# Reordering both ends of a two-layer attention kernel: query and key blocks in turns, timetables of their own for three sequences, and a last tree in two halves

## The chip, the core and the metric

The kernel runs on one core of a Trainium2 chip. The metric is the device time of one execution in microseconds (us). Five engines work side by side, each through its own queue in program order: PE (TensorE, matmuls; PEld in the profile is its weight load), DVE (VectorE), ACT (ScalarE), POOL (GpSimd) and SP (SyncE, which here issues all DMA transfers).

## What is computed

The input is x, 8 sequences of 512 tokens with 256 features, all float32. Two layers follow each other, each an attention and a soft decision tree, both with a residual:

```python
x = x + attn_a(layernorm(x))   # 16 heads of 16, with biases, no mask
x = x + ffn(layernorm(x))
x = x + attn_b(layernorm(x))   # 16 heads of 16, rotary positions, causal
x = x + ffn(layernorm(x))

def ffn(x):                    # a tree of depth 8: 255 inner nodes, 256 leaves
    q = einsum('btd,ed->bte', x, Wq)
    gate = sigmoid(q @ routers.T)
    leaf_prob = product of the gates, or of one minus them, along each path
    return einsum('btd,ed->bte', leaf_prob @ leaf_values, Wout_w) + Wout_b
```

## The kernel before

**Sequences and steps.** The kernel counts sixteen sequences: 0 to 7 are the batch in the first layer, 8 to 15 the same batch in the second (causal) layer. A sequence has 32 ticks (`STEPS`): four groups of four heads, four steps in each group, two ticks per step. In one step (the loop at L655) the program writes, in this order, the transposed scores of one block of 128 keys and their exponentials (`scores`, tiles `st` and `pt`), and the row maxima of one block of 128 queries that are needed seven steps later (`maxima`, tiles `mx` and `most`; `LEAD` is 14 ticks). After the fourth step of a group, `weigh` multiplies the exponentials by the values (`av`). The maxima of four steps are negated and transposed (`less`, `lessT`), and moved to the tile `m`, from which a third matmul adds them to the scores.

**Banks.** All matmul results go to eight PSUM banks that are handed out in turn. A step takes four for `st` and four for `mx`, so the next scores need banks that the exponentials on ACT, and the reductions on DVE, have let go.

**Fillers.** Everything else is put between these steps by a small planner (`Units`). A generator yields the kind of its next piece and the tick from which it is due: "big" and "small" are PE pieces (pulled once per step, after `weigh`), "v" is DVE, "g" POOL (both pulled twice), "d" a DMA, "row" the transposed maxima. A piece that is due is written at the next pull of its kind, the oldest due time first. The engines' queues then hold exactly the order of the program (`in_program_order`). The due times come from two tables: `BEFORE` (what a sequence needs before its steps, relative to its own start) and `BEHIND` (what follows its attention, relative to the next sequence's start), each with one entry for the first layer and one for the causal layer.

**Before its steps** (`pre`, L355), a sequence loads x (`x`), takes the statistics (`stats`, DVE), normalizes (`norm`, POOL: L284 to L292, tile `xn`), transposes (`xt`), and makes queries and keys in two blocks of 128 features each (`q`, `k`, L403). In the first layer ACT writes each block twice, as float32 (`r`) and rounded (`hl`, first half), and `halves` (L329) subtracts them for the second half of `hl` (`q_halves`, `k_halves`). `move` then issues four DMAs for a query block and two for a key block, of 256 KB each, which bring the features of a head together in the tiles `q` and `k`. `hl` has two buffers. The values (`v`) and the residual's bias (`bias`, POOL) follow.

**Behind its steps**, `spread` moves the outputs and the softmax sums, `divide` (L542) makes the reciprocals, sends them through DRAM and back (`apart`, `den`), and multiplies (L555). `post` makes the output projection (`y`), which is added to x (L562), and `tree` (L578) the rest: statistics, norm (`xnt`), transposes (`txt`), gates (`z`, `th`), the products down the tree (`levels`, tile `lp`, two DVE instructions for each of eight levels), transposes (`lt`), the leaf product (`ty`) and the store. A tree takes up to two sequences' time, so those of two sequences are in flight together.

**At the start**, sequence 0 runs through `pre` alone, then its values, then its moves; the four products of the tree's constant weights (`chains`, tiles `wg` and `wl`) begin at tick 2, and the value bias is folded into the output bias (`fold_bias`) at the end of `pre`. **At the end**, the planner is drained one tick at a time (L680).

Of the kernel before, what the change touches and what calls it, by code (L numbers as in the profile page):

```python
# [41 lines left out]
F32 = mybir.dt.float32  # L42
# [6 lines left out]
P = 128  # L49
B, S, D = 8, 512, 256  # L50
H, HD = 16, 16
# [17 lines left out]

BEFORE = (  # L70
    dict(x=-41, stats=(-39, -39), norm=(-34, -34, -34), xt=(-33, -29), q=(-29, -27), k=(-27, -27),
         q_halves=(-27, -27), k_halves=(-23, -23), v=(-13, -13, -11, -11), bias=(-12, -6)),
    dict(x=-43, stats=(-42, -39), norm=(-37, -37, -37), xt=(-33, -33), q=(-29, -27), k=(-19, -19),
         q_turn=(-25, -22), q_round=-20, q_halves=(-20, -20), k_turn=(-18, -17), k_round=-17,
         k_halves=(-17, -17), v=(-13, -13, -9, -9)),
)
BEHIND = (
    dict(y=(11, 11, 15, 15), stats=(15, 18), norm=(18, 18, 18), xt=(23, 23), z=(27, 29, 29, 29),
         bias=(30, 30), levels=(31, 32, 39, 39, 39, 41), lt=(43, 53), ty=(63, 63, 67, 67)),
    dict(y=(13, 13, 15, 15), stats=(18, 19), norm=(19, 19, 20), xt=(25, 27), z=(29, 29, 29, 29),  # L80
         bias=(20, 25), levels=(30, 30, 31, 34, 40, 40), lt=(47, 51), ty=(53, 53, 63, 69)),
# [3 lines left out]
OUTPUT = (3, 1, 2, 1, 3)  # L85

# [47 lines left out]
def hybrid_kernel(ctx, tc, x, a_qk, a_v, a_o, a_qk_b, a_v_b, a_o_b, b_q, b_k, b_v, b_o,  # L134
# [33 lines left out]
    def store_x(n):  # L168
        dst = between[n] if n < B else out[n - B]
        nc.sync.dma_start(dst.rearrange("(t p) d -> p t d", p=P), xs.pop(n))  # L170
# [8 lines left out]
    for m in ms:  # L179
# [23 lines left out]
        for w, n, tag in ((f_q, "f_q", "lpT"), (f_routers, "f_routers", "th"),  # L203
                          (f_values, "f_values", "lp"), (f_out, "f_out", "den"))
# [22 lines left out]
    units = Units()  # L227
    wg = const.tile([P, NC, NODES], F32, tag="wg", name="wg")
    wl = const.tile([P, NC, D], F32, tag="wl", name="wl")

    def chains():


        for to, left, right in ((wg, raws[0], raws[1]), (wl, raws[2], raws[3])):
            n = to.shape[2]
            for m in range(NC):
                ps = bank([P, D], f"w{n}_{m}")
                for k in range(NC):
                    nc.tensor.matmul(
                        ps[:, :n], lhsT=left[:, k, m * P : (m + 1) * P], rhs=right[:, k, :],  # L240
                        start=k == 0, stop=k == NC - 1,
                    )
                if to is wl:
                    nc.vector.tensor_scalar(to[:, m, :], ps[:, :n], leaf_scale[:, m : m + 1], None, ALU.mult)
                else:
                    nc.scalar.copy(to[:, m, :], ps[:, :n])
                yield "big", units.now + 2

    def fold_bias():

        vb = pool1.tile([P, NC, P], F32, tag="lp1", name="vb")
        for c in range(NC):
            nc.vector.tensor_copy(vb[:, c, :], v_b[:, c : c + 1].to_broadcast([P, P]))
        ps = bank([P, D], "vbo")
        for c in range(NC):
            nc.tensor.matmul(ps, lhsT=vb[:, c, :], rhs=wa.o[:, c, :], start=c == 0, stop=c == NC - 1)
        nc.vector.tensor_tensor(out_b, ps, out_b, ALU.add)

    def before(n, name):

        return shifted(BEFORE[n >= B][name], n)

    def behind(n, name):

        return shifted(BEHIND[n >= B][name], n + 1)
# [5 lines left out]
    def layer_norm(n, name, when, got):  # L271

        x = xs[n]
        stats = pool2.tile([P, NT, 6], F32, tag="ln_stats", name=f"ln_stats{name}")
        mv = pool2.tile([P, NT, 2], F32, tag="ln_mv", name=f"ln_mv{name}")
        for t in range(NT):
            if t == 2:
                yield "v", when(n, "stats")[1]
            nc.vector.bn_stats(stats[:, t, :], x[:, t, :])
            nc.vector.bn_aggr(mv[:, t, :], stats[:, t, :])  # L280
        times = when(n, "norm")
        yield "g", times[0]
        less_mean = pool2.tile([P, NT], F32, tag="ln_less", name=f"ln_less{name}")
        nc.gpsimd.tensor_scalar(less_mean, mv[:, :, 0], -1.0, None, ALU.mult)  # L284
        rstd = pool2.tile([P, NT], F32, tag="ln_rstd", name=f"ln_rstd{name}")
        nc.gpsimd.tensor_scalar(rstd, mv[:, :, 1], EPS, None, ALU.add)
        nc.gpsimd.tensor_tensor(rstd, rstd, neg_half, ALU.pow)
        xn = pool2.tile([P, NT, D], F32, tag="xn", name=f"xn{name}")
        for t in range(NT):
            if t % 2 == 0:  # L290
                yield "g", times[1 + t // 2]
            nc.gpsimd.tensor_scalar(  # L292
                xn[:, t, :], x[:, t, :], less_mean[:, t : t + 1], rstd[:, t : t + 1], ALU.add, ALU.mult
            )
        got.append(xn)

    def add_bias(n, bias, times):
        for t in range(0, NT, 2):
            part = xs[n][:, t : t + 2, :]
            nc.gpsimd.tensor_tensor(part, part, bias.unsqueeze(1).to_broadcast([P, 2, D]), ALU.add)  # L300
            if t == 0:
                yield "g", times[1]
# [8 lines left out]
    def by_tokens(srcT, w, n, name, evict, times):  # L311


        t = 0
        while t < NT:
            if t:
                yield "big", times[t]
            count = 2 if t < NT - 1 and times[t] == times[t + 1] else 1
# [8 lines left out]
            t += count  # L327

    def halves(raw, hl, which, n, c):  # L329


        on = nc.vector if n >= B else nc.gpsimd
# [20 lines left out]
        moves.setdefault(n, []).append(units.add(move(), "d", units.now + 1))  # L353

    def pre(n):  # L355
# [33 lines left out]
        vals[n] = units.add(by_tokens(xnT, w.v, D, f"v{n}", values, times), "big", times[0])  # L389
        for which, name in enumerate("qk"):  # L390
# [3 lines left out]
            for c in range(NC):  # L394
                yield "big", before(n, name)[c]
                if not which and not c:

                    assert before(n, name)[0] > (n - 1) * STEPS + LEAD
                    qs[n] = [pool2.tile([P, NG, S], F32R, tag=f"q{i}", name=f"q{i}_{n}") for i in range(2)]
                    ks[n] = pool2.tile([P, NG, S], F32R, tag="k", name=f"k{n}")  # L400
# [7 lines left out]
                if causal:  # L408

                    for i, table in enumerate((cos, sin) if c == 0 else (sin, cos)):  # L410
                        raws.append(pool1.tile([P, S], F32, tag=f"r{c}{i}", name=f"r{n}{which}{c}{i}"))
                        nc.vector.tensor_tensor(raws[-1], ps, table, ALU.mult)
                else:
                    raws.append(pool1.tile([P, S], F32, tag=f"r{which}{c}", name=f"r{n}{which}{c}"))
                    at = 2 * which + c
                    for to in (raws[c], hls[c][:, 0, :]):
                        nc.scalar.activation(to, ps, AF.Identity, bias=w.qk_b[:, at : at + 1])  # L417
# [10 lines left out]
        if n == 0:  # L428
            fold_bias()

# [111 lines left out]
    def divide(n, c):  # L542
# [11 lines left out]
        yield "g", units.now + OUTPUT[4]  # L554
        nc.gpsimd.tensor_tensor(outT[:, c, :], outT[:, c, :], den, ALU.mult)  # L555
# [10 lines left out]
    def post(n):  # L566
# [9 lines left out]
        yield from tree(n)  # L576

    def tree(n):  # L578

        got = []
        yield from layer_norm(n, f"t{n}", behind, got)
        xn = got[0]
        for c in range(NC):
            yield "small", behind(n, "xt")[c]
            if c == 0:
                xnT = pool2.tile([P, NC, S], F32, tag="xnT", name=f"txnT{n}")
            transposed(xnT, xn, c, f"txt{n}_{c}")
        times = behind(n, "bias")  # L590
        biases[n] = units.add(add_bias(n, f_bias, times), "g", times[0])
        yield "big", behind(n, "z")[0]
        if n:
            units.finish(trees[n - 1], lambda: paths[0] == n - 1)
        th = pool1.tile([P, NT, LEAVES], F32, tag="th", name=f"th{n}")
# [6 lines left out]
        yield from by_tokens(xnT, wg, NODES, f"z{n}", gates, behind(n, "z"))  # L602

        lp = None
        times = deque(behind(n, "levels"))
        for level in range(DEPTH):
            m = 1 << level
            for side, one in enumerate((-1.0, 1.0)):
                if level == DEPTH - 1 or (side == 0 and level in (0, 3, 5, 6)):
                    yield "v", times.popleft()  # L610
                if side == 0:
                    if level == DEPTH - 1 and n:
                        units.finish(trees[n - 1], lambda: paths[1] == n - 1)
                    new = pool1.tile([P, NT, 2 * m], F32, tag=f"lp{level % 2}" if level < DEPTH - 1 else "lp",
                                     name=f"lp{n}_{level}")
                    pairs = new.rearrange("p t (n s) -> p t n s", s=2)
                    of_level = th[:, :, m - 1 : 2 * m - 1]
                if lp is None:
                    nc.vector.tensor_scalar(pairs[:, :, :, side], of_level, one, None, ALU.add)
                else:  # L620
                    nc.vector.scalar_tensor_tensor(  # L621
                        pairs[:, :, :, side], of_level, one, lp, ALU.add, ALU.mult
# [3 lines left out]
        for c in range(NC):  # L626
            yield "small", behind(n, "lt")[c]
            if c == 0:
                if n:
                    units.finish(trees[n - 1])  # L630
                lpT = pool1.tile([P, NC, S], F32, tag="lpT", name=f"lpT{n}")
            transposed(lpT, lp, c, f"lt{n}_{c}")
        paths[1] = n
        yield "big", behind(n, "ty")[0]
        yield from by_tokens(lpT, wl, D, f"ty{n}", to_x(n), behind(n, "ty"))
        yield "d", units.now + 2
        units.finish(biases.pop(n))
        store_x(n)
# [11 lines left out]
    units.finish(vals.pop(0))  # L650
    for move in moves.pop(0):
        units.finish(move)
    units.add(chains(), "big", 2)
# [99 lines left out]
```

## Time and profile before

| What | us |
|---|---|
| median of three runs | 1194.44 |
| lowest and highest | 1192.46, 1198.91 |
| profiled execution, its own time | 1199.47 |
| its span, from the first to the last instruction | 1197.8 |
| PE busy in the span | 1089.3 (91%) |
| DVE busy | 842.1 (70%) |
| ACT busy | 639.8 (53%) |
| POOL busy | 405.9 (34%) |
| first matmul of the maxima | 28.30 |
| first matmul of the scores | 47.01 |
| last copy of an attention output (`o`) begins | 1152.77 |
| last addition to x begins | 1193.47 |

All times of the trace are counted from the start of the span. A busy engine is one that has an instruction under way; a matmul's end is modelled, so a busy PE isn't PE at its peak. The granted clock is the share of PE's full clock in a stretch: it is a mean of pieces at 1.0 and at 0.5. Where a line of the timeline or of the chain of waits has a bracket, it is the idle time of the engine before that instruction, and what ended it.

The distance from one sequence's first exponential to the next one's is some 70 to 74 us in the first layer and 66 to 72 in the causal layer; from the first one of sequence 15 to the end of its last it is 51.7 us.

### The profile page before, as it was taken

Reading aid. Unit: us, or ns where it says so; the run is one execution under the profiler, and the core shown is the slowest. Engines: PE = TensorE matmul, PEld = TensorE weight load, DVE = VectorE, ACT = ScalarE, POOL = GpSimd, SP = SyncE. Lnnn points to the kernel's source line nnn. Section 1 sums busy time; section 2 is a strip of 40 time slices with the busy share of each in tenths; the row PEclk is TensorE's granted clock in tenths of the full one; section 3 lists DMA queues with packets and bytes.
Section 4 is the critical chain, followed back from the end, with each engine's and each line's share of the span. In section 5 each row is a group of like instructions: output and inputs, shape, how many; then the busy total and the mean of one; then the engine's idle time right before and its main releaser. Section 6 shows DMA issues by size and latency. Waiting matters only on the chain. (4 is left out here: it accounts for less than half of the span.)

```text
span 1197.8 us, 24647 instructions
## 1 busy us (share of the span) xinstructions
PE 1089.3 (91%) x8916; PEld 619.1 (52%) x8916; DVE 842.1 (70%) x2384; ACT 639.8 (53%) x1451; POOL 405.9 (34%) x636
## 2 busy tenths in 40 slices
PE   5999999999999999999998999999989988899966
PEld 3434354555535545454554555555564645555544
DVE  2866487777767777777767787777878777776723
ACT  2266667666657566665663544545453544544431
POOL 4121223232422214232233443435453543434332
PEclk9689999999999999999998999989999999989988
DMA  8020302104141131411302214031312313030110
GB/s 285 6 112 21 120 21 82 56 16 143 38 138 39 35 116 39 143 60 38 133 18 108 74 38 148 32 124 33 134 49 80 103 34 143 30 126 16 41 50 35
DMA packets 69658, 91.52 MB, mean 76 GB/s; under 512 B 15008, under 2 KB 36256, under 8 KB 69536
## 3 DMA queue, kind: packets, MB, share of 16 engines
q1 hardware_dynamic: 69536, 89.94, 21.7%
q8 instruction: 70, 1.15, 0.4%
q14 instruction: 52, 0.43, 0.1%
HBM read 20.71 MB, written 8.91 MB: 25 GB/s over the span
## 5 line engine op out<-in xcount | busy, mean ns | idle before, releaser
L499 ACT ACTIVATE pt<-st 128x512 f32<-128x512 f32 (+3 forms) x1024 | 446.8, 523 | 198.5 <-PE st L436 195.1
L463 DVE TENSOR_REDUCE most<-mx 128x1 f32<-128x512 f32 x512 | 317.3, 683 | 134.8 <-PE mx L436 134.6
L458 DVE CUSTOM_DVE_ANT_0 seen<-mx,mask 128x384 f32<-128x384 f32 (+3 forms) x512 | 251.0, 490 | 123.4 <-PE mx L436 66.9
L436 PE MATMUL mx<-k,q 32*128 32x512 f32 (+3 forms) x2048 | 241.1, 400 | 42.1 <-DMA k<-hl 9.0
L515 PE MATMUL av<-pt,v 128*32 128x512 f32 (+3 forms) x2048 | 213.6, 561 | 5.7 <-ACT pt L499 3.8
L436 PE MATMUL st<-q,k 32*128 32x512 f32 (+3 forms) x2048 | 198.5, 410 | 1.6 <-ACT pt L499 0.8
L502 POOL TENSOR_SCALAR_AFFINE_SELECT pt<-pt 128x256 f32<-128x256 f32 x256 | 105.4, 424 | 278.4 <-ACT pt L499 274.4
L436 PEld LDWEIGHTS mx<-k,q 32*128 32x128 f32 x2048 | 136.3, 187 | 107.5 <-DVE x L562 22.6
L436 PEld LDWEIGHTS st<-q,k 32*128 32x128 f32 x2048 | 94.3, 186 | 114.6 <-issue 73.4
L515 PEld LDWEIGHTS av<-pt,v 128*32 128x32 f32 x2048 | 65.6, 117 | 141.9 <-issue 109.4
L520 ACT COPY o<-av 128x512 f32<-128x512 f32 x64 | 37.6, 587 | 161.4 <-issue 124.3
L436 PE MATMUL st<-m,ones 32*128 32x512 f32 (+3 forms) x1024 | 104.1, 358 | 0.0
L333 POOL TENSOR_TENSOR hl<-r,hl 128x512 fp32r<-128x512 f32 x32 | 41.5, 1297 | 166.1 <-ACT hl L417 166.1
L621 DVE SCALAR_TENSOR_TENSOR lp<-th,lp 128x8 f32<-128x8 f32 (+6 forms) x224 | 66.8, 336 | 2.6
L555 POOL TENSOR_TENSOR out<-out,den 128x512 f32<-128x512 f32 x32 | 41.6, 1299 | 76.0 <-DMA den<-apart 73.9
L322 PE MATMUL z<-wg,txnT 128*128 128x255 f32 x256 | 63.6, 396 | 3.0 <-ACT pt L499 2.6
L403 PE MATMUL qk<-xnT,b_qk 128*128 128x512 f32 x128 | 64.4, 638 | 1.5 <-ACT pt L499 0.8
L403 PE MATMUL qk<-xnT,a_qk 128*128 128x512 f32 x128 | 64.6, 636 | 0.2
L322 PE MATMUL ty<-wl,lpT 128*128 128x256 f32 x256 | 63.8, 388 | 0.5 <-ACT lpT L309 0.2
L436 PEld LDWEIGHTS st<-m,ones 32*128 32x128 f32 x1024 | 59.4, 187 | 5.7
L284 POOL TENSOR_SCALAR ln_lesst<-ln_mvt 128x4 f32<-128x4 f32 x16 | 3.8, 239 | 162.6 <-DVE ln_mvt L280 162.6
L322 PEld LDWEIGHTS z<-wg,txnT 128*128 128x128 f32 x256 | 47.5, 194 | 15.1 <-ACT pt L499 7.1
(76 smaller groups left out, 1136.5 us busy)
## 6 DMA issues: line engine op xcount, KB each, us to landing
q<-hl SPq DMA_DIRECT2D x128, 256.0 KB
k<-hl SPq DMA_DIRECT2D x64, 256.0 KB
out<-o SPq DMA_DIRECT2D x64, 128.0 KB
den<-apart SPq DMA_DIRECT2D x32, 256.0 KB
x<-x SPq DMA_DIRECT2D x8, 512.0 KB
between<-x SPq DMA_DIRECT2D x8, 512.0 KB
x<-between SPq DMA_DIRECT2D x8, 512.0 KB
out<-x SPq DMA_DIRECT2D x8, 512.0 KB
```

The source lines that it names most:

```text
L322: nc.tensor.matmul(ps[:, i, :n], lhsT=srcT[:, c, (t + i) * P : (t + i + 1) * P], rhs=w[:, c, :], start=c == 0, stop=c == NC - 1,)
L333: on.tensor_tensor(hl[:, 1, :], raw, hl[:, 0, :].bitcast(F32), ALU.subtract)
L403: nc.tensor.matmul(ps, lhsT=wt[:, k, c * P : (c + 1) * P], rhs=xnT[:, k, :], start=k == 0, stop=k == NC - 1,)
L436: nc.tensor.matmul(ps, lhsT=lhsT, rhs=rhs, start=i == 0, stop=i == len(operands) - 1)
L458: nc.vector.tensor_tensor_reduce(out=seen[:, :width], in0=ps[:, :width], in1=mask[:, S - width :], scale=1.0, scalar=LOWEST, op0=ALU.add, ...
L463: nc.vector.tensor_reduce(at, ps, AX.X, ALU.max)
L499: nc.scalar.activation(pt[:, i, : S - first], ps[:, : S - first], AF.Exp, scale=SCALE)
L502: nc.gpsimd.affine_select(out=pt[:, :, :P], in_=pt[:, :, :P], pattern=[[0, 2], [1, P]], compare_op=ALU.is_ge, fill=0.0, base=0, channel_mu ...
L515: nc.tensor.matmul(av[32 * j : 32 * j + 32, first:], lhsT=vs[n % 2][:, kt, g * NJ + j, :, :].rearrange("p d s -> p (d s)"), rhs=pts[j // 2 ...
L520: nc.scalar.copy(o4, av)
L555: nc.gpsimd.tensor_tensor(outT[:, c, :], outT[:, c, :], den, ALU.mult)
L621: nc.vector.scalar_tensor_tensor(pairs[:, :, :, side], of_level, one, lp, ALU.add, ALU.mult)
```

## The change

**Start.** `pre(0)` makes the blocks in the order q0, k0, q1, k1, and each is moved as soon as it is made. The second blocks' `hl` lie in the two buffers of `out`, so four buffers serve. The key blocks' subtraction goes to DVE. The norm of sequence 0 is on DVE, but for the power (still POOL). The values of sequence 0 are no longer finished ahead of the loop; they have ticks 7, 7, 11 and 11. `fold_bias` (its copies now on POOL) and the four weight products move from the start to the ticks 25, 27, 29, 43 and 49.

**Timetables.** Sequences 0 and 1 get entries of their own in `BEFORE`; several due times of the two common entries change. Sequence 14 gets its own entry in `BEHIND`, and the halves of sequence 15 one each.

**End.** For sequence 15 the division is done by DVE in two halves of 256 tokens. Each half starts its own `last`: projection, statistics, norm, one bank of transposes for its two tiles, gates, levels, leaf product and store. The second half has tiles of its own, in buffers of `hl`, `r` and `out`.

```diff
+LAST = 2 * B - 1
 BEFORE = (
-    dict(x=-41, stats=(-39, -39), norm=(-34, -34, -34), xt=(-33, -29), q=(-29, -27), k=(-27, -27),
-         q_halves=(-27, -27), k_halves=(-23, -23), v=(-13, -13, -11, -11), bias=(-12, -6)),
-    dict(x=-43, stats=(-42, -39), norm=(-37, -37, -37), xt=(-33, -33), q=(-29, -27), k=(-19, -19),
-         q_turn=(-25, -22), q_round=-20, q_halves=(-20, -20), k_turn=(-18, -17), k_round=-17,
-         k_halves=(-17, -17), v=(-13, -13, -9, -9)),
+    dict(x=-47, stats=(-39, -39), norm=(-34, -34, -34), xt=(-33, -29), q=(-29, -27), k=(-27, -27),
+         q_halves=(-27, -27), k_halves=(-27, -27), v=(-13, -13, -11, -11), bias=(-16, -10)),
+    dict(x=-43, stats=(-42, -42), norm=(-39, -37, -37), xt=(-33, -33), q=(-29, -27), k=(-19, -19),
+         q_turn=(-26, -24), q_round=-20, q_halves=(-20, -20), k_turn=(-18, -17), k_round=-17,
+         k_halves=(-17, -17), v=(-11, -11, -9, -9)),
+    dict(x=-41, stats=(-41, -39), norm=(-37, -32, -32), xt=(-31, -31), q=(-29, -27), k=(-23, -19),
+         q_halves=(-23, -23), k_halves=(-19, -19), v=(-13, -11, -5, -3), bias=(-8, 6)),
+    dict(v=(-7, -7, -3, -3), bias=(13, 18)),
 )
 BEHIND = (
-    dict(y=(11, 11, 15, 15), stats=(15, 18), norm=(18, 18, 18), xt=(23, 23), z=(27, 29, 29, 29),
-         bias=(30, 30), levels=(31, 32, 39, 39, 39, 41), lt=(43, 53), ty=(63, 63, 67, 67)),
-    dict(y=(13, 13, 15, 15), stats=(18, 19), norm=(19, 19, 20), xt=(25, 27), z=(29, 29, 29, 29),
-         bias=(20, 25), levels=(30, 30, 31, 34, 40, 40), lt=(47, 51), ty=(53, 53, 63, 69)),
+    dict(y=(11, 11, 15, 15), stats=(15, 18), norm=(18, 18, 19), xt=(23, 23), z=(27, 29, 29, 29),
+         bias=(30, 34), levels=(31, 32, 36, 39, 39, 41), lt=(43, 53), ty=(63, 63, 67, 67)),
+    dict(y=(13, 13, 15, 15), stats=(18, 19), norm=(23, 23, 23), xt=(25, 27), z=(29, 29, 29, 29),
+         bias=(18, 30), levels=(30, 30, 31, 34, 39, 41), lt=(47, 51), ty=(53, 53, 63, 69)),
+    dict(y=(5, 5, 15, 15), stats=(15, 15), norm=(15, 15, 16), xt=(19, 23), z=(27, 27, 31, 31),
+         bias=(20, 25), levels=(31, 31, 32, 34, 40, 40), lt=(47, 47), ty=(53, 53, 63, 63)),
+    dict(y=(15, 15), stats=18, norm=(18, 21), xt=21, z=(29, 29), bias=28,
+         levels=(29, 29, 35, 38, 38, 38), lt=43, ty=(49, 49)),
+    dict(y=(19, 19), stats=20, norm=(21, 28), xt=29, z=(39, 39), bias=39,
+         levels=(46, 46, 47, 47, 48, 48), lt=51, ty=(53, 53)),
 )
+CHAINS = (25, 27, 29, 43, 49, 49)
...
     def before(n, name):
-        return shifted(BEFORE[n >= B][name], n)
+        table = BEFORE[(3, 2)[n] if n < 2 else n >= B]
+        return shifted(table[name] if name in table else BEFORE[0][name], n)
     def behind(n, name):
-        return shifted(BEHIND[n >= B][name], n + 1)
+        return shifted(BEHIND[2 if n == LAST - 1 else n >= B][name], n + 1)
...
+        on = nc.vector if name == "n0" else nc.gpsimd
...
     def halves(raw, hl, which, n, c):
-        on = nc.vector if n >= B else nc.gpsimd
+        on = nc.vector if n >= B or (n == 0 and which) else nc.gpsimd
...
+        if n == 0:
+            queries_and_keys(n)
+            for c in range(NC):
+                for which in range(2):
+                    raw, hl = block(w, xnT, which, c, "out" if c else "hl")
+                    halves(raw, hl, which, n, c)
+                    units.finish(moves[n][-1])
+            return
...
-        if n == 0:
-            fold_bias()
...
+        if n == LAST and c == NC - 1:
+            for half in range(2):
+                part = slice(half * S // 2, (half + 1) * S // 2)
+                nc.vector.tensor_tensor(outT[:, c, part], outT[:, c, part], den[:, part], ALU.mult)
+                units.add(last(half), "big", shifted(BEHIND[3 + half]["y"], n + 1)[0])
+            return
...
+    def transposed_half(dst, src, ts, name):
+        ps = bank([P, NC, 2, P], name)
+        for c in range(NC):
+            for i, t in enumerate(ts):
+                nc.tensor.transpose(ps[:, c, i, :], src[:, t, c * P : (c + 1) * P], ident)
+        nc.scalar.copy(dst[:, :, ts[0] * P : ts[0] * P + 2 * P], ps.rearrange("p c t q -> p c (t q)"))
...
+    def last(half):
+        ts = range(2 * half, 2 * half + 2)
+        def when(n, name):
+            return shifted(BEHIND[3 + half][name], n + 1)
+        yield from by_tokens(outs[LAST][0], wb.o, D, f"y{LAST}", to_x(LAST), when(LAST, "y"), ts)
+        yield "v", when(LAST, "stats")
+        yield from tree(LAST, when, ts)
...
     units.finish(pres.pop(0))
-    units.finish(vals.pop(0))
-    for move in moves.pop(0):
-        units.finish(move)
-    units.add(chains(), "big", 2)
+    moves.pop(0)
+    units.add(chains(), "big", CHAINS[0])
```

## The prediction

> **What bounds the kernel now.** I read the page's 40 slices first, then the busy time by stretches, then the timeline of the first 50 us, one step of the first sequence, and the chain of waits from the last softmax to the end. In the slices the matmul engine is at nine tenths or more except at both ends.
>
> ```profile
> PE   5999999999999999999998999999989988899966
> PEclk9689999999999999999998999989999999989988
> ```
>
> The second row is the granted clock in tenths. The middle is PE-bound at nearly full clock; idle time that a new order can fill lies at the two ends. The start, in the timeline (start, length, engine, line, work, and in brackets the idle time before it and what ended it):
>
> ```profile
> 23.64 0.69 ACT L417 ACTIVATE hl<-qk,a_qk_b 128x512 fp32r<-128x512 f32 x1 [3.14 <-DMA q<-hl]
> 24.35 4.58 SPq L346 DMA_DIRECT2D k<-hl  x4
> 28.30 1.21 PE L436 MATMUL mx<-k,q 32*128 32x512 f32 x16 [2.50 <-DMA k<-hl]
> ```
>
> The first key block is written at 23.64 because `hl` has two buffers and both hold queries that are still being moved; its moves leave from 24.35, and the first maxima start at 28.30, when they land. Then the lead, and the cold steps after it:
>
> ```profile
> 28.30:47.00 18.70, 15.70 (x77) 8.56 (x77) 17.49 (x36) 1.00 (x3) 6.22 (x10) 0.72 0.08 29
> 47.00:57.00 10.00, 10.00 (x49) 5.85 (x49) 7.86 (x15) 5.56 (x11) 0.00 (x0) 0.50 0.01 2
> ```
>
> Columns: stretch, its length, busy us of PE, weight loads, DVE, ACT, POOL, granted clock, DMA share, GB/s. In the lead DVE is busy 17.49 of 18.70 us: it sets the pace. The end, in the chain of waits (start, length, what):
>
> ```profile
> 1157.92 3.56 DMA den<-apart
> ...
> 1161.64 1.27 POOL out L555
> ...
> 1162.96 2.93 PE y L322 x6
> ...
> 1173.09 2.19 POOL xnt L292 x4
> ...
> 1176.65 5.30 PE z L322 x16
> ...
> 1187.36 1.94 PE lt L308 x8
> 1189.30 4.14 PE ty L322 x16
> ```
>
> From 1153.4, when the last `av` is out, to 1197.8 one tree runs through PE, DVE, POOL, PE, ACT, DVE, PE in turn: 44 us with one engine working at a time.
>
> **First blocks in turns: -3.2 us at the first maxima.** Before, SP issued eight query moves, then four of keys. The trace's landings of the query moves lie 0.68 us apart, from 21.51 to 26.16: a full DMA queue, behind the loads of `sin` (landed 20.83). The two moves of the first key block landed at 26.79 and 28.06. After: q0 (4 moves), k0 (2), q1 (4), k1 (2), with four buffers, so nobody waits for one. Is q0 ready in time? The norm of sequence 0 goes from POOL to DVE but for the power. POOL's four `xn` took 2.18 us. For DVE the nearest row is `wl`, one 128x256 scaling, 476 ns, but it reads PSUM. The Trainium skill ("VectorE: DVE Perf Modes", the perf-mode tier table) gives fp32 tensor_scalar in SBUF two elements a cycle, which I work out as some 0.3 us (estimate). By the row 4 x 0.48 = 1.9 us, by the rule 1.2: q0 starts 0.3 or 1.0 us earlier than its 12.65. Then 3.7 us of cold matmul (12.65 to 16.37), two evictions of 0.68, POOL's half of 1.27: q0's four moves are issued from about 17 to 19.5, k0's (its half now on DVE, 0.73 us) by 20.5. Both answers end ahead of the queue: q0's moves still land at 21.5 to 23.5, two of 0.68 us more give 24.9, and the maxima start at 25.1 instead of 28.3. So rule and row give the same sum here, since the DMA queue decides; the DVE norm itself is worth nothing. Bounds: 0 if the queue is slower behind smaller gaps, -5 if loads drain sooner; I take -3.2.
>
> **The lead: -1.0 us.** DVE's sum is 6 groups x 4 reductions x 0.61 = 14.7, the statistics of sequence 1 (2.3), `less` (0.35), and two `wl` scalings (0.96). The first scores take the banks of the sixth group, so they wait for this sum: 29.03 + 18.3 = 47.3 against 47.01 measured. The scalings leave the lead. The values' 16 matmuls (3.6 us, free until now in the wait for the moves) enter it, beside PE's gaps: of 18.7 us PE is busy 15.7 with 6.3 us of weight products that go away, so they are covered. If that cover failed they'd cost 3.6. The transposes of sequence 1 move behind the first scores; they waited for POOL until 45.97 right ahead of them. First scores at 42.8 instead of 47.0: -4.2 in all.
>
> **First sequence: +0.5.** It receives the bias fold (4 matmuls) and four weight products (16 matmuls). Warm they take 20 x 0.21 = 4.3 us (16 `v` matmuls took 3.62 us with the clock up). A step without filler looks like this:
>
> ```profile
> 78.55 1.71 PE L436 MATMUL st<-q,k 32*128 32x512 f32 x8 [0.20 <-ACT pt L499]
> 80.31 2.06 ACT L499 ACTIVATE pt<-st 128x512 f32<-128x512 f32 x4 [0.72 <-PE st L436]
> 83.21 1.09 ACT L499 ACTIVATE pt<-st 128x512 f32<-128x512 f32 x2 [0.83 <-PE st L436]
> ```
>
> The exponentials start 2.9 us apart; PE's eight matmuls take 1.71 us here and 0.75 at 76.42: 0.9 us of every such step is PE waiting for banks. So a filler of 0.86 us is hidden, and only what exceeds 0.9 costs. Sequence 1's two key blocks (1.72 us each, both in one step before, which lasted 7.2 us) now go to two steps, and its `v` to four steps of one tile rather than two of two. Sum of max(0, filler - 0.9) over the sixteen steps: before about 1.4 + 0.8 + 2.5 + 1.5 (the `av`) + 1.6; after 0.3 + 0.8 + 0.8 + 1.5 + 1.7 + 1.7 + 0.8: equal within 0.3. POOL's two copies of the bias stand behind 2.5 us of query halves; PE's fold is queued behind them with the next scores after it: up to 0.5. I take +0.5; bounds -3 (fewer cold slices than the 10 us from 47 to 57) and +4.3 (no cover).
>
> **Timetables of sequences 2 to 14: 0.** In the first layer from sequence 2 on PE's order is unchanged; POOL and DVE items move by one or two steps, key halves are made one step earlier, inputs are loaded six ticks earlier, past few others in SP's queue. In the causal layer `v` moves one step, into the next lighter one (3.1 us after one of 3.9), the tree's norm three or four ticks later, and its bias adds are split. PE's gaps over 0.5 us from 130 to 1100 sum to some 25 us, most of them bank waits that nothing here touches: a gain of 4 is the most, and a loss of 4 the range I keep.
>
> **The tail in halves: -8.** The factor `den` lands at 1161.5 as before. DVE multiplies half the tokens in 0.42 us (the row of 128x256 adds) where POOL took 1.27: y0 starts at 1162.1, not 1162.96. `lt` of tree 14, which stood between the two `y` at 1165.7, is now ahead of both, in the 8.8 us in which PE waits for `den`. Half 0 then: y, 8 matmuls, cold to 1165.8 (six took 2.93); add 0.7 and two statistics 1.05: 1167.5; POOL's three small steps 1.6[...] and two `xn` 1.1: 1170.3; transposes 0.7 and copy 0.7: 1171.7; z, 8 matmuls, 1.8: 1173.5; tanh 0.6, levels 2.9 (the pairs of 3.9 us at half the elements, by the next smaller rows): 1177.1; lt, copy, ty 1.3 + 1.8: 1180.3. Half 1 follows: its y to 1168, statistics after half 0's, POOL done 1172.8, z after half 0's z and the rest of `ty` of tree 14 at 1177.5, tanh and levels (DVE just free) 1181.2, lt and copy 1182.6, ty 1184.4, or 1186 if cold, add 0.7. So the last add ends at 1185 to 1187 instead of 1193.9: -7.5. The last store moves two tiles instead of four: 0.7 us less at the 0.68 us per 256 KB of the start. Together -8.
>
> **The rule that speaks against.** The Trainium skill ("TensorE: Matmul & The Clock Gate", Part 1) says PE's clock halves after an idle window of about 3.4 us[...]. The rows agree on the halving: 8 `y` warm at 1166.5 took 1.89 us; the 16 `z` at 1176.5, after 2.66 us of idling and transposes, 5.47. The tail's matmuls need some 16 us warm and 31 cold. Were all cold, PE itself would bound the halves from 1162.1: with its two waits for POOL the last add is at 1195.8, and the gain gone. But halves close the gaps (the longest I find is 0.7 us), and the run of y, y, ty begins at the time when it brought the clock up before. I go by the row; the cold case is a rival.
>
> **Sum.** -4.2 + 0.5 + 0 - 8 = -11.7. The profiled execution took 1199.47 (span 1197.8 and 1.7 around it), so it would take 1187.8; it lies 5.0 above the runs' median of 1194.44, and carried over the median becomes 1182.7.
>
> **Rivals.** *Cold or uncovered PE* (0.18): the tail gains 4 instead of 8 and the first sequence pays the 4.3 of its new matmuls: -4.2 + 4.3 - 4 = -4, 1190.5. For it: clock 0.50 from 47 to 57. *Steady gain as well* (0.17): the POOL burst in each causal sequence (bias adds, norm, division: 953.9 to 961.7 in one) is split, `av` and `y` stop waiting, first sequence warmer: -18, 1176. Against: `av` waited for POOL 6.4 us in the whole run. *Late norm, slower* (0.06): the causal tree's norm goes to tick 23, its transposes stay at 25. In one sequence `xn` ended at 945.8 and the transposes began at 950.4; two steps later, behind the masks, I get 948.9, 1.5 us of slack. If POOL comes over 3.2 us later than that, 1.7 us of stall in each of seven sequences eats the gain; at 3 us each it is +21 - 11.7: 1204. *The halves don't overlap* (0.04), if tiles are tracked whole: the tail gains 1, 1190. The forecast has 0.55, own range 1178 to 1188.
>
> Change from no change is told apart at 0.5%, 6 us: faster means under 1188.5. The forecast brings 0.53, the steady gain 0.17, the cold case 0.05 and the halves 0.01: faster 0.76; same 0.17; slower 0.07. For 8 in 10 the range reaches half into both sides: 1174 to 1191.
>
> **What would show it.** First `mx` at 25 and first `st` at 43, with `most` back to back between; the steps of sequence 0 without one of 7 us; 70 us for each first-layer and 67 to 69 for each causal sequence as before; the last `av` to the end in 36 us; `z` of the halves at 0.21 to 0.24 us a matmul. A `txt` in the causal layer that waits on `xnt`, a fold that waits on POOL, or a tail at 0.4 us a matmul would prove it wrong.

## The result

The changed kernel takes 1182.6 us (median of five runs, 1181.03 to 1186.97) against 1194.44: a ratio of 0.9891, with a 95% interval from 0.9855 to 0.9928. A second set of runs of both kernels gave 0.9855 (0.9808 to 0.9902). The forecast of 1182.7 is a ratio of 0.990; it lies in the first interval and at the edge of the second. The ratios compare undisturbed runs only and are not quotients of the medians (that is 0.9901 in the first set). The profiled execution took 1183.02 us with a span of 1181.3.

The same rows of the page, of the changed kernel:

```profile
PE   5999999999999999999998999998999988899976
PEclk8899999999999999999998899989998988999898
```

PE is as full as before. In the first three slices the clock is 8, 8 and 9 where it was 9, 6 and 8; the last two slices of PE are no emptier, there are merely fewer microseconds of them. The start, in the timeline of the changed kernel:

```profile
18.34 1.21 SPq L386 DMA_DIRECT2D k<-hl  x2
19.64 0.74 SPq L388 DMA_DIRECT2D q<-hl  x1
...
23.24 7.19 PE L499 MATMUL mx<-k,q 32*128 32x512 f32 x32 [3.77 <-DMA k<-hl]
```

The first keys are moved between the two query blocks, at 18.34 instead of 24.35, and the first maxima start at 23.24. They still wait for the keys, 3.77 us. The end, in its chain of waits:

```profile
1149.80 3.60 DMA den<-apart
1154.01 6.30 PE y L361 x14
1163.15 2.01 PE z L361 x8
1172.30 1.99 PE ty L361 x8
1175.41 2.01 PE ty L361 x8
```

The gates of a half take 2.01 us for 8 matmuls, so the clock is up, where the 16 of the whole tree took 5.30. The 14 matmuls of `y` behind `den` take 6.30: from 1154.0 to 1160.4 the granted clock is 0.52, so this stretch is cold.

Where the time went is seen when the execution is cut at events that all kernels share: the first matmul of the maxima, the first exponential of sequences 0, 1, 8 and 15, and the last copy of an attention output. Each cell is the stage's length in us; after the stroke stands the time in it at half clock. The experiments below explain the names.

| trace | to first maxima | lead, to first exponential | sequence 0 | 1 to 7 | 8 to 14 | 15 | tail | span |
|---|---|---|---|---|---|---|---|---|
| before | 28.3 | 20.8 / 12 | 70.5 / 22 | 500.8 / 10 | 478.1 / 41 | 54.3 / 7 | 45.0 / 21 | 1197.8 |
| before_again | 27.1 | 20.4 / 7 | 74.4 / 33 | 498.8 / 7 | 480.9 / 44 | 55.4 / 10 | 46.2 / 21 | 1203.3 |
| changed | 23.2 | 19.3 / 14 | 64.6 / 3 | 499.5 / 7 | 481.2 / 58 | 56.7 / 14 | 36.7 / 11 | 1181.3 |
| after_again | 23.4 | 18.6 / 7 | 64.4 / 3 | 500.7 / 10 | 480.1 / 58 | 56.7 / 14 | 36.8 / 11 | 1180.6 |
| no_halves | 23.0 | 18.6 / 10 | 67.9 / 14 | 499.3 / 7 | 480.4 / 58 | 56.7 / 14 | 46.8 / 21 | 1192.5 |
| plain_order | 27.9 | 19.1 / 11 | 64.2 / 3 | 501.2 / 10 | 471.8 / 34 | 55.5 / 10 | 36.8 / 11 | 1176.4 |
| early_fill | 27.2 | 19.7 / 4 | 65.7 / 13 | 499.6 / 7 | 474.4 / 44 | 56.7 / 14 | 36.8 / 11 | 1180.0 |
| old_seq1 | 23.6 | 19.1 / 10 | 69.7 / 14 | 496.5 / 0 | 481.9 / 61 | 54.5 / 10 | 36.7 / 11 | 1182.0 |
| old_tables | 23.2 | 18.6 / 10 | 62.6 / 0 | 500.8 / 10 | 477.5 / 38 | 54.9 / 14 | 38.0 / 15 | 1175.6 |
| old_14 | 23.4 | 19.1 / 10 | 64.2 / 3 | 500.8 / 10 | 477.2 / 48 | 56.6 / 10 | 37.0 / 11 | 1178.2 |
| more_buffers | 24.3 | 19.6 / 10 | 64.3 / 3 | 498.7 / 3 | 478.4 / 51 | 56.1 / 17 | 36.6 / 11 | 1178.0 |
| pool_norm | 24.6 | 19.1 / 10 | 64.1 / 3 | 500.1 / 10 | 481.2 / 58 | 55.3 / 10 | 37.5 / 14 | 1181.9 |
| split_all | 23.2 | 20.1 / 17 | 64.5 / 3 | 504.4 / 7 | 484.4 / 65 | 56.7 / 14 | 36.7 / 11 | 1190.0 |
| key_buffers | 23.1 | 18.6 / 10 | 66.1 / 7 | 493.7 / 0 | 486.6 / 72 | 56.8 / 14 | 36.7 / 11 | 1181.4 |

Three stages gain most: the time to the first maxima, sequence 0, and the tail; the lead gains 1.6 us. The gain of sequence 0 is not in the prediction.

### The profile page after: what moved, and what is told of

It is laid out like the page before. It is cut to its first block, busy times and chain, and to the rows that moved or that the text cites. A ratio compares the mean times of both kernels' runs of the same rounds, so it can differ in the third digit from the quotient of the medians.

```text
span 1181.3 us, 24706 instructions
## 1 busy us (share of the span) xinstructions
PE 1079.5 (91%) x8916; PEld 621.1 (53%) x8916; DVE 840.4 (71%) x2406; ACT 640.1 (54%) x1451; POOL 401.3 (34%) x632
## 4 chain that ended last, share of the span: by engine, by line
PE 65%; DVE 14%; ACT 7%; issue 5%; DMA 4%; POOL 3%; SPq 1%; DVEq 0%; ACTq 0%; POOLq 0%
PE av L578 15%; PE st L499 13%; PE mx L499 8%; DVE seen L521 6%; ACT pt L562 6%; PE z L361 5%; PE v L361 4%; PE ty L361 4%; PE y L361 4%; PE qk L475 4%; PE qk L403 3%; DMA q<-hl 2%; DVE most L526 2%; PE lt L335 1%; DMA k<-hl 1%
## 5 line engine op out<-in xcount | busy, mean ns | idle before, releaser
L499 PE MATMUL mx<-k,q 32*128 32x512 f32 (+3 forms) x2048 | 238.4, 399 | 43.4 <-DMA k<-hl 10.1
L499 PE MATMUL st<-q,k 32*128 32x512 f32 (+3 forms) x2048 | 193.5, 409 | 1.3 <-ACT pt L562 0.4
L499 PEld LDWEIGHTS mx<-k,q 32*128 32x128 f32 x2048 | 136.6, 187 | 106.2 <-DVE most L521 24.3
L475 PE MATMUL qk<-xnT,b_qk 128*128 128x512 f32 x128 | 64.5, 639 | 1.8 <-ACT pt L562 1.0
L718 DVE SCALAR_TENSOR_TENSOR lp<-th,lp 128x8 f32<-128x8 f32 (+7 forms) x238 | 63.8, 305 | 2.6
L443 ACT COPY v<-v 128x256 f32<-128x256 f32 x64 | 21.6, 389 | 67.8 <-PE v L361 67.6
L361 PEld LDWEIGHTS ty<-wl,lpT 128*128 128x128 f32 x256 | 48.0, 195 | 14.6 <-issue 5.9
```

Source lines behind the costliest of these rows:

```text
L361: nc.tensor.matmul(ps[:, i, :n], lhsT=srcT[:, c, (t + i) * P : (t + i + 1) * P], rhs=w[:, c, :], start=c == 0, stop=c == NC - 1,)
L475: nc.tensor.matmul(ps, lhsT=wt[:, k, c * P : (c + 1) * P], rhs=xnT[:, k, :], start=k == 0, stop=k == NC - 1,)
L499: nc.tensor.matmul(ps, lhsT=lhsT, rhs=rhs, start=i == 0, stop=i == len(operands) - 1)
L718: nc.vector.scalar_tensor_tensor(pairs[:, :, :, side], of_level, one, lp[:, part, :], ALU.add, ALU.mult)
```

## The experiments

Single executions of one kernel differ by 1 to 2% in these runs, so that times alone can't tell parts of a few microseconds apart. Much of this goes with the clock: of six executions of the changed kernel in one set, the shortest, 1170.16 us, had a mean granted clock of 0.971, the longest, 1184.61, one of 0.952. So each part is judged by its stage in a trace, mostly one trace per kernel; the times stand beside them.

**A second trace of before.**

> The kernel before, unchanged, for a second trace. The first sequence (from its first exponential to that of sequence 1) took 70.5 us in the first trace of before, with 21.7 us at half clock, and 64.6 in the changed kernel, with 3.4. If the clock there is chance, this trace shows some 65 to 67 us and under 12 us at half clock; if it belongs to the old order (a lead with idle PE before it), it shows 69 to 71 and 18 or more again. First maxima at 28.3 if the initial loads are always that slow; at 26.5 if the loads' 1.7 us was chance.

Sequence 0 took 74.4 us with 33 us at half clock, and the first maxima started at 27.14. So the long first sequence belongs to the old order. The loads were quicker here: `sin` landed at 18.59, and at 20.83 in the first trace; the 28.30 had some chance in it. This execution took 1205.03 us, the median of before in that set of runs was 1199.73.

**The tail.**

```diff
-        if n == LAST and c == NC - 1:
+        if False:
```

> The changed kernel with the last tree in one piece, as before, the rest of the change kept. By the sum of the prediction the tail (from the last copy of an attention output to the end) is 8 us longer: 45 instead of 36.7, and the time 1190.6. If the halves gain nothing of their own and the tail got shorter because the last tree but one has left it, it is 2 us or less longer: 1184.6.

The tail is 46.8 us instead of 36.7: the halves are worth 10 us. The time is 1188.13, a ratio of 0.9895 (0.9864 to 0.9927). In its chain of waits:

```profile
1150.96 3.46 DMA den<-apart
1155.90 2.93 PE y L361 x6
1160.54 2.17 PE y L361 x8
1167.42 2.19 POOL xnt L316 x4
1170.98 5.58 PE z L361 x16
1182.02 1.94 PE lt L335 x8
1183.96 4.26 PE ty L361 x16
```

It is the chain of before again: 16 `z` in 5.58 us, 16 `ty` in 4.26, each after a pause. With halves, 8 of each take 2.0, and the rest of the time runs beside the other half. Half clock in the tail falls from 21 us to 11.

**The start.** Two parts were undone, each alone. First the order of the blocks:

```diff
-        on = nc.vector if n >= B or (n == 0 and which) else nc.gpsimd
+        on = nc.vector if n >= B else nc.gpsimd
...
-            for c in range(NC):
-                for which in range(2):
-                    raw, hl = block(w, xnT, which, c, "out" if c else "hl")
-                    halves(raw, hl, which, n, c)
-                    units.finish(moves[n][-1])
+            for which in range(2):
+                made = [block(w, xnT, which, c, "hl") for c in range(NC)]
+                for c in range(NC):
+                    halves(*made[c], which, n, c)
...
-    moves.pop(0)
+    for move in moves.pop(0):
+        units.finish(move)
```

So the two buffers, the moves at the end and the keys' subtraction on POOL come back together; this run doesn't part them.

> The changed kernel with the first blocks made and moved as before (q0, q1, k0, k1, two buffers, moves at the end, subtractions on POOL). If the turns are what the earlier first maxima come from, those start 3 to 3.5 us later than in the changed kernel and everything shifts by as much: 1185.8. If the norm on DVE or the loads brought it, under 1 us: 1183.

Then the place of the values, the fold (its copies on DVE again) and the weight products:

```diff
-        fold_bias()
-        times = deque(CHAINS[1:])
-        yield "big", times.popleft()
...
-                yield "big", times.popleft()
+                yield "big", units.now + 2
...
-            nc.gpsimd.tensor_copy(vb[:, c, :], v_b[:, c : c + 1].to_broadcast([P, P]))
+            nc.vector.tensor_copy(vb[:, c, :], v_b[:, c : c + 1].to_broadcast([P, P]))
...
                     units.finish(moves[n][-1])
+            fold_bias()
             return
...
+    units.finish(vals.pop(0))
     moves.pop(0)
-    units.add(chains(), "big", CHAINS[0])
+    units.add(chains(), "big", 2)
```

> The changed kernel with the values of sequence 0 finished ahead of the maxima, the fold at the end of its blocks and the four weight products from tick 2, as before. If their place is worth nothing (the prediction: lead -1.0 by the weight scalings that leave it, first sequence +0.5), first sequence 64 and the time within 1 us: 1182 to 1183.5. If the fillers in the first sequence keep PE's clock up, that sequence shows 10 us or more at half clock and takes 69 to 71: 1187 to 1189.

With the old order the maxima start at 27.91, 4.6 us later than the mean of the two traces of the changed kernel (1.3 us of it may be the loads, whose `sin` landed at 20.6 here); with the old place of the fillers at 27.20, 3.9 later. Each alone undoes the gain at this point. PE's timeline of the second (early_fill) says why:

```profile
22.69 1.13 PE L272 MATMUL vbo<-a_o,vb 128*128 128x256 f32 x4 [2.22 <-DVE vb L269]
23.66 3.62 PE L358 MATMUL v<-a_v,xnT 128*128 128x256 f32 x16
27.20 1.54 PE L497 MATMUL mx<-k,q 32*128 32x512 f32 x16
```

By the trace's landings the keys were there at 22.8, but PE's queue still held the fold, which waits 2.22 us for DVE, and the 16 value matmuls. Those were free in the old wait for the keys, and would have been the next bound. The times are 1183.51 and 1183.31 (ratios 0.988, 0.984 to 0.9921, and 0.9878, 0.9827 to 0.9928); in their traces both had less time at half clock in sequences 8 to 14 (34 and 44 us) than the changed kernel's (58), which hides the 4 us. Sequence 0 kept its gain in both (64.2 and 65.7): it comes neither from the turns nor from the fillers.

**The norm on DVE.**

```diff
-        on = nc.vector if name == "n0" else nc.gpsimd
+        on = nc.gpsimd
```

> The changed kernel with the norm of sequence 0 on POOL again. By the prediction it is worth nothing, since the full DMA queue and not the blocks decides when the first keys land: first maxima at 23.0 to 23.8. If the blocks decide, the first query block is evicted 1 to 1.2 us later and the maxima start at 24.3 to 24.8.

The maxima start at 24.57, in the range of the other theory, but the landings give another reason. By the trace's landings, the last move of the first keys landed 4.08 us after `sin` (20.45, then 24.53); in the changed kernel's two traces 4.06 and 4.02 (19.13, 23.19 and 19.35, 23.36): six transfers of 0.68 us each time. The first query move was issued at 16.68, and at 16.54 in after_again, where the maxima started 1.2 us earlier. What was later is the load of `sin`; it varies between executions with the norm on POOL too (18.6 and 20.8 in the two traces of before). The run more_buffers, described below, settles it from the other side: with the norm on DVE and the first query move issued at 15.71, its `sin` landed at 20.13 and its maxima started at 24.25. In all eleven traces with the blocks in turns the first keys landed 4.0 to 4.1 us behind `sin`, while the first query move was issued anywhere from 15.5 to 16.7. So the norm is worth nothing here, as forecast. This execution took 1183.59 us.

**Sequence 0.**

```diff
-        table = BEFORE[(3, 2)[n] if n < 2 else n >= B]
+        table = BEFORE[(3, 0)[n] if n < 2 else n >= B]
```

> The changed kernel with sequence 1 on the common timetable, so that its two key blocks stand in one step again and its values in two pairs. If that timetable is what shortens the first sequence (it stayed at 65.7 us when the weight products and values left it), it takes 69 to 72 us here, one step of it 7 us or more, and the kernel 4 to 6 us longer. If the clock after the start decides, and not the timetable, it takes 64 to 66 us with under 4 us at half clock.

It took 69.7 us, and the kernel 1182.94 (ratio 0.9873, 0.9818 to 0.9928) beside 1178.69 of the changed kernel in the same set. So the timetable of sequence 1 shortens sequence 0. ACT's timeline of the step of 7.3 us, and PE's:

```profile
63.96 0.69 ACT L411 ACTIVATE hl<-qk,a_qk_b 128x512 fp32r<-128x512 f32 x1 [1.42 <-DMA q<-hl]
64.55 2.05 ACT L562 ACTIVATE pt<-st 128x512 f32<-128x512 f32 x4
64.70 0.82 PE L499 MATMUL mx<-k,q 32*128 32x512 f32 x5 [1.76 <-ACT hl L411]
65.45 5.18 PE L578 MATMUL av<-pt,v 128*32 128x512 f32 x32
```

ACT waits 1.42 us to write the second key block: of the two buffers of `hl` one holds the first key block, the other the second query block, whose last move lands only at 63.89. The exponentials of the step stand behind it in ACT's queue, PE waits 1.76 us for a bank, and 32 `av` matmuls then take 5.18 us. It is the kind of wait that held up the start, one sequence later. To see whether it is the buffers, or just two blocks in a step, the key blocks got two buffers of another tile, with the old timetable left in place:

```diff
-                    raw, hl = block(w, xnT, which, c, "hl")
+                    raw, hl = block(w, xnT, which, c, "out" if which and n == 1 else "hl")
```

> The changed kernel with sequence 1 on the common timetable, as in the run old_seq1, but with its two key blocks in the buffers of another tile, so that they need not wait for the moves of its queries. If that wait (ACT idle 1.4 us in front of the second key block, the exponentials of a whole step behind it) is what its own timetable removes, the step of 7.3 us falls to 6 to 6.4 and the first sequence takes 64.5 to 67 instead of 69.7. If two key blocks in one step cost by their matmuls and evictions alone, the step stays over 7 and the sequence at 69 or more.

```profile
62.71 0.68 ACT L411 ACTIVATE hl<-qk,a_qk_b 128x512 fp32r<-128x512 f32 x1
63.28 2.06 ACT L562 ACTIVATE pt<-st 128x512 f32<-128x512 f32 x4
64.10 3.64 PE L578 MATMUL av<-pt,v 128*32 128x512 f32 x32
```

No wait, 5.7 us instead of 7.3 for the step, 5.4 instead of 7.0 for the next, 3.64 for the same `av`; sequence 0 takes 64.3, as with the timetable of its own, and the one execution 1179.68. So spreading the two key blocks brings nothing beside the removal of the wait: the timetable makes the keys two and four steps later, when the buffers are free.

The two steps make up 3.2 of the 5.3 us. The rest goes with the clock: half clock falls from 14 to 3 us. One of the stretches of old_seq1, from 65.2 to 68.6, follows the wait at once and lies in the two steps. But another runs from 44.7 to 51.5, ahead of the wait, and one starts at 106.2, some 40 us behind it. That these belong to the wait is not shown: no_halves, which has no such wait in sequence 0, has 14 us at half clock there too, and takes 67.9.

**The other timetables.** First the two common entries of `BEFORE` and of `BEHIND`, all of their due times as in the kernel before:

```diff
...
-         q_halves=(-27, -27), k_halves=(-27, -27), v=(-13, -13, -11, -11), bias=(-16, -10)),
+         q_halves=(-27, -27), k_halves=(-23, -23), v=(-13, -13, -11, -11), bias=(-12, -6)),
...
-    dict(y=(13, 13, 15, 15), stats=(18, 19), norm=(23, 23, 23), xt=(25, 27), z=(29, 29, 29, 29),
+    dict(y=(13, 13, 15, 15), stats=(18, 19), norm=(19, 19, 20), xt=(25, 27), z=(29, 29, 29, 29),
...
```

> The changed kernel with the due times of before in the two common entries (sequences 2 to 13). By the prediction they are worth nothing: sequences 1 to 14 take 974 to 981 us together, as in all traces so far. If they bring what the traces suggest at equal time at half clock (the changed tables some 4 us less), 1 to 14 take 978 to 983 with some 50 us at half clock, and the kernel is 3 to 5 us slower than the changed one.

Sequences 1 to 14 took 978.3 us with 48 us at half clock; the changed kernel's two traces have 980.7 and 980.8 with 65 and 68. At like time at half clock the new entries are shorter: in sequences 8 to 14 they have 471.8 at 34 us and 474.4 at 44 us, the old ones 477.5 at 38, 478.1 at 41 and 480.9 at 44, some 5 us more. But the new ones mostly show more time at half clock (ten traces with these sequences as changed: 34 to 65, mean 54; three with the old entries: mean 41). A line through the ten rises by 0.40 us for each us at half clock, which gives 5 back. Times: 1181.01, a ratio of 0.9885 (0.9846 to 0.9924), beside 1178.69 of the changed kernel in the same set. Whether the clock loss belongs to the new entries is left open. In the changed kernel the causal transposes start after `xn` each time (in sequence 11 the tile `xnt` is ready at 936.1, `txt` starts at 937.4; 1.3 to 1.8 us lie between them in sequences 8 to 13): the late norm doesn't hold them up.

```diff
-        return shifted(BEHIND[2 if n == LAST - 1 else n >= B][name], n + 1)
+        return shifted(BEHIND[n >= B][name], n + 1)
```

> The changed kernel with sequence 14 on the common timetable. In all traces with its own one, sequence 15 took 55.5 to 56.7 us to the last copy of its outputs, before 54.3 and 55.4. If its own timetable costs that, sequence 15 takes 54 to 55.5 here and the tail 1 to 2 us more than 36.7, since the transposes and leaf products of 14 come back into it: time within 1.5 us of the changed kernel. If the tail needs it, the tail is 39 or more and the kernel 2 us slower.

Sequence 15 took 56.6 and the tail 37.0; 1179.65 us, ratio 0.9861 (0.9818 to 0.9904). Sequence 14's own timetable is worth nothing that these runs can tell; neither expectation held. Why sequence 15 takes two us more than before stays open: half clock alone isn't it, since old_14 has 56.6 us with 10 at half clock and before_again 55.4 with as much.

**The changed kernel again.**

> The changed kernel, unchanged, beside the others of this set. First maxima at 23 to 23.5, first sequence 64 to 68, tail 36.7 to 36.9, as in the kernels that share these parts; time 8 to 17 us under before on the same chip. If the first trace of the changed kernel was a lucky one, the first sequence shows 69 or more.

All stages came back within 1.2 us.

**Two attempts to go on.** Spreading the key blocks of sequences 2 to 7 as well:

```diff
-         k=(-27, -27), q_halves=(-27, -27), k_halves=(-27, -27),
+         k=(-23, -19), q_halves=(-23, -23), k_halves=(-19, -19),
```

> The changed kernel with the key blocks of sequences 2 to 7 spread over two later steps as well, as sequence 1 has them. If two key blocks in one step cost more than one in each of two steps in every sequence (0.9 us of each step hidden), sequences 1 to 7 take 494 to 496 us instead of 499 to 501 and the kernel 5 us less. If only sequence 1 is hurt, because its queries are moved late, they stay at 498 to 501; if the keys now land too late for the next sequence's maxima, they take over 502.

Sequences 1 to 7 took 504.4 us, 4 more; 1183.88, ratio 0.9874 (0.9843 to 0.9906). The cause isn't the late landing that the expectation names: PE's waits for keys sum to 9.4 us, against 8.9 in after_again. In sequence 2 the four steps in question took 5.7, 5.4, 3.0 and 3.6 us in after_again (17.7), and 3.0, 5.5, 4.8 and 5.7 here (19.0): two key blocks in one step cost 2.7 us there, and one in each of the two later steps 1.8 and 2.1. Nothing like 0.9 us of a block is hidden in those two. Last, the buffers for all sequences:

```diff
-                    raw, hl = block(w, xnT, which, c, "hl")
+                    raw, hl = block(w, xnT, which, c, "xn" if which else "hl")
```

(and the same in the causal layer).

> The changed kernel with the key blocks of sequences 1 to 15 in the buffers of `xn`, which lie idle at that time. In the traces of the changed kernel ACT still waits four times for the moves of query blocks in front of a key block (at 128, 341, 570 and 715 us, 0.9 to 1.7 us each). If these waits hold up whole steps as the one in sequence 0 did, all four go, the step of 7.2 us in sequence 1 falls to 5.7 to 6.3, sequences 1 and 4 take 69.5 to 70.7 each, and the time is 4 to 7 us under the changed kernel's: a ratio to before of 0.981 to 0.985. If the norm's next use of `xn` then waits for the moves, or the waits were hidden, nothing is gained: 0.9855 to 0.989.

None of the four waits is left. The two steps of sequence 1 that took 7.2 and 7.0 us in the changed kernel take 5.7 and 5.4, the same gain as in sequence 0. Sequence 1 took 68.3 us instead of 71.3 and 72.6 in the changed kernel's two traces, sequence 4 70.8 instead of 72.3 and 73.7, and sequences 1 to 7 together 493.7 instead of 500. Of these 6 us some 3 are the waits themselves: old_seq1, which had two of them in this stage and no time at half clock either, took 496.5. In busy time by stretches (length, then PE, weight loads, DVE, ACT, POOL, clock), sequences 1 to 7, and sequences 8 to 14:

```profile
107.70:601.40 493.70, 471.90 (x3877) 256.31 (x3873) 360.38 (x795) 320.09 (x646) 139.74 (x166) 1.00 0.22 75
601.40:1088.00 486.60, 446.84 (x3890) 272.06 (x3883) 356.83 (x1295) 233.25 (x616) 208.69 (x372) 0.93 0.22 78
```

The clock is never down in the first; in the second it is down for more time than in any other trace, 72 us, which gives the 6 us back in this execution of 1183.14. The ratio is 0.9805 (0.9754 to 0.9857), but it rests on four of six executions, one of them of 1165.48 us. The medians, 1179.96 against 1198.22, have the quotient 0.985, as in the changed kernel's second set (0.986). That this kernel is faster than the changed one is not shown.

## Why the prediction was right, and where its terms were off

The sum was -11.7 us, the medians moved by 11.8. That the hit is so close is luck: the second set of times moved by 17.1, and the stages, as means of two traces each, by 19.5. Some 3 us of the latter lie in the choice of executions: those traced of before were 5.0 and 5.3 us above the medians of their sets, those of the changed kernel 0.4 and 3.7. Two large terms held, a third of the same size was missed.

| step of the prediction | forecast | measured (mean of two traces each) |
|---|---|---|
| first maxima | -3.2 | -4.4 |
| lead | -1.0 | -1.6 |
| first sequence | +0.5 | -7.9 |
| sequences 1 to 14 | 0 | +1.4 |
| sequence 15 | 0 | +1.9 |
| tail | -8 | -8.9 |

**First maxima: right in mechanism.** The full DMA queue set the landing of the keys, six transfers of 0.68 us behind `sin`; the forecast of 25.1 was that sum, from a `sin` at 20.83. It landed at 19.1 and 19.4, and the keys 4.06 and 4.02 us later. The rival reading, that the issues set this pace (they too are some 0.65 us apart), is ruled out by the landings of pool_norm and more_buffers, which follow `sin` and not the first issue. The four `xn` on DVE took 1.38 us, near the 1.2 by the rule and not the 1.9 by the row; as forecast, it made no difference. In before the keys weren't bound by the queue but by their buffers, so quicker loads gain less there (28.3 and 27.1). The prediction treated the values as covered in the lead; early_fill shows that they had to leave the start for the turns to gain anything.

**Lead: right in size,** within the spread of 18.6 to 19.3. That it was the two scalings isn't told apart: early_fill, which puts them back, has 19.7, and traces without them reach 20.1.

**First sequence: the wrong term.** The prediction counted what PE's fillers exceed 0.9 us by, step by step, and found both orders equal. It saw the step of 7.2 us with two key blocks, but put 3.4 of it down to their matmuls. The trace of before had more, in its list of waits and in ACT's timeline:

```profile
ACT hl L417 <- DMA q<-hl: 8.5, 5, 3.1
69.84 0.69 ACT L417 ACTIVATE hl<-qk,a_qk_b 128x512 fp32r<-128x512 f32 x1 [1.35 <-DMA q<-hl]
```

ACT waited five times, 8.5 us in all, for the moves of queries in front of a block, and one of these waits, 1.35 us, stood in this step. It is the same kind of wait that the prediction reads at the start of the kernel, and it wasn't looked for again. It and the cold matmuls behind it account for 3.2 of the 7.9 us (old_seq1 against more_buffers). No run accounts for the other 4.7 alone; they go with less time at half clock (22 and 33 us in before, 14 in old_seq1, 3 in the changed kernel), and why there is less stays open. One sign of the prediction failed with it: a step of 7.1 us is left in the first trace of the changed kernel, with half clock from 57.6 to 61.1; the second has 5.6 there. That 0.9 us of a filler is hidden was read from one step without fillers; split_all shows that it doesn't hold for two others.

**Timetables: 0 stands, within what can be told.** At equal clock they gain something like 5 us, a little over the bound of 4 that was kept, and the clock took about as much. The late norm didn't come: its slack, put at 1.5 us, was 1.3 to 1.8.

**Tail: right,** by its own chain. Counted from the last copy of an output, the last addition begins after 32.9 us instead of 40.7: 7.8 less where 7.5 was forecast. Behind it another 0.8 went, where 0.7 was put down to the smaller store. POOL's three small steps took 1.3 us for a half where 1.6 was counted (the power 0.72 us on 128x2, 1.04 on 128x4). In the first trace the clock rose with the closed gaps, as the rows promised: `y`, behind pauses of PE of 3.10 and 3.72 us, was cold, and `z` took 2.0 us for 8. In the second a stretch of 3.4 us at half clock came again at 1162.8, and the first eight `z` took 2.92. The all-cold case was worked out from the Trainium skill ("TensorE: Matmul & The Clock Gate", Part 1), by which the clock halves after an idle window of about 3.4 us. It did not come: 11 of the tail's 37 us were at half clock in both traces, and between the matmuls of the halves PE's longest pause was 1.91 us.

## What to carry to other kernels

When a step lasts longer than its matmuls explain, look at every engine's wait in it, and look for a wait found once in all places where the same buffers turn over: a write held up by a DMA on an in-order engine holds up all work queued behind it. A chain over several engines at the end of a kernel can be worth splitting in two (10 us here), even when no engine is busy in it. A wait that is removed at the start of a kernel is worth only what stands behind it in the same queue allows, so move that as well.

## What the runs showed of the hardware

**The clock.** Time at half clock goes with much of the scatter here. The same code in sequences 8 to 14 took 471.8 us with 34 us at half clock (plain_order) and 481.2 with 58 (changed); over the 14 traces it sums to 83 to 123 us. What sets it in the causal layer isn't settled.

**The queue.** With the blocks in turns, the first keys landed 4.0 to 4.1 us behind `sin` in each of eleven traces: six transfers of 256 KB, 0.68 us each, though the first was issued anywhere from 15.5 to 16.7.

**A wait in front of queued work.** A pause of 1.4 us in ACT cost 3.2 us over two steps (old_seq1 against more_buffers), since the `av` behind it took 5.18 us instead of 3.64, partly at half clock.
